# Performer attention with a mixture of experts: row means of three normalisations as product columns, variances as ScalarE squares with row sums, and two buffers for turned tokens

## The chip, the cores and the metric

The kernel runs on one core of a Trainium2 chip. Its engines work side by side, each through its own instructions in order: PE (TensorE, matrix products), DVE (VectorE), ACT (ScalarE), POOL (GpSimd) and SP, which here issues DMAs. They wait for each other through semaphores. The metric is the device time of one execution in microseconds (us), the median of several. All numbers are float32, save in small parts of the expert choice.

## The reference, cut to what matters

There are 4096 tokens of 256 numbers, as 8 sequences of 512. What is computed:

```python
# x: (8, 512, 256)
a = layernorm(x)                                      # norm "a"
q, k, v = a @ Wq.T + bq, a @ Wk.T + bk, a @ Wv.T + bv # 16 heads of 16
kp, qp = softmax_kernel(k), softmax_kernel(q)         # 64 features per head, exp(xp - diag - max) + eps
attn = ((qp @ (kp^T v)) / (qp @ sum(kp))) @ Wo.T + bo
r = layer_norm(a + attn, g2, be2)                     # norm "b"
r = layer_norm(r + relu(r @ W1.T + b1) @ W2.T + b2, g3, be3)   # norm "c"
x = x + layernorm(r)                                  # norm "d"
xf = layernorm(x)                                     # norm "e"
scores = softmax(xf @ gate_w.T)                       # 8 experts
# every expert takes its 512 best tokens: norm, 256 -> 1024 -> 256, weighted, added to xf
x = x + layernorm(xf)
```

For keys the maximum in `softmax_kernel` runs over all 512 tokens and 64 features of a head, so no key can be exponentiated before the whole sequence's features are known. A norm needs each row's mean and variance. Since a row of `r @ W2.T` and its mean are both linear in `r @ W1.T` and so on, the gate's scores are already computed through extra columns of the products (below).

## The kernel before, in words

**Tiles.** 128 tokens lie on the partitions. A block is one sequence: `NB` = 8 blocks of `NT` = 4 tiles. Weights stay in SBUF; `D` = 256, hidden width `FF` = 1024 in `NF` = 8 pieces, `E` = 8 experts.

**Stages.** The attention stage, with the first MLP and the norms a to e, runs up to about 594 us of the profile. The choice of tokens follows, up to about 650, and then the experts with gather, products and scatter.

**Order.** The attention stage's instructions are put out by `planner` (line 187). Each task has an engine, a weight (its expected time), a place (a due time; block b's places lie 66 further on for each block, `COURSE`) and the tasks that it follows. The planner goes through time: of an engine's tasks that can start first, it takes the one with the lowest place. The result is a fixed order for each engine. PSUM buffers are taken as "mm" (three, for most products), "px" (one, for raw features) and "sm" (one).

**The chain of a block**, by tile names and lines. Norm a gives `xnx`. PE turns it (`TX`, line 544), ACT copies it to `xnT` (548), which has one buffer. Products of it give `pk`, `pq` (564) and `pv` (688); ACT makes `kT` and its squares (574, 575) and `v_aug` (699), DVE copies the gate columns out of `pv` (task GA, 707). `pd` and `pnt` (588, 603) are the squared norms. Raw features `pxk` and `pxq` (627) share the one "px" buffer. DVE takes maxima and subtracts (XK: 646, 649), takes the maximum over tiles (`mxt`, 662); POOL reduces it over the partitions (`mxa`, 670), DVE negates it (`nstab`, 677). Then ACT exponentiates keys (724), DVE adds the small constant (KE, 730) and PE forms the context `pc` (744). For queries DVE finds maxima and subtracts (XQ: `sh` 807, `qd` 814), ACT exponentiates (QE, 826), PE turns (`ptq`, 833), ACT copies to `qpT` (844), PE forms `pdiv` and `po` (864, 874), `pr` (909) and, from `atT` (917), `pw` (932). RW (941) adds `pw` to `xnx` in `r1x`. Norm b follows, `TA` (544) and `xaT` (550), the MLP's `ph` (951), `hT` on ACT (956, task PHe) and `pm` (1004), MA (1016) adds `pm` in `r1x`; then the norms c, d and e, and `xf` on ACT (175).

**A norm** is `stats` (two DVE instructions for each tile, lines 153 and 154), `root` (two on POOL for all four tiles, 157 and 158) and an affine of two DVE instructions a tile (166, 169), or a plain one (161), `centre` and `scaled_plus` (180, 183). In `normalisation` the tasks are letter + S, R and A:

```python
def stats(st, mv, src, i):
    nc.vector.bn_stats(st[:, i, :], src[:, 0:D])
    nc.vector.bn_aggr(mv[:, i, :], st[:, i, :])
```

**Gate columns.** Weight tiles carry further columns beside their 256: `wv_sb` 16, `wo_sb` and `w2_sb` 8. So `pv`, `pw` and `pm` carry each token's share of the gate's scores, which norms then only shift and scale: the tasks G0 to G4, small operations on POOL (lines 471 to 512 hold their helpers). XB (1358) is one POOL addition of the attention's bias to the whole block of `xnx`.

**The last block** has nothing after it. `last_mlp` (1155) works it tile by tile: steps L 1 to 4 on DVE (first, second, third, fourth) with a root on POOL after each of the first three. `scores`, turned as `pT` (1438), begins the choice.

## Time and profile before

| what | us |
| --- | --- |
| median of three runs | 897.42 (897.06 to 898.75) |
| the profiled execution, its own time | 899.18 |
| its span | 897.5 |
| mean granted clock of PE | 0.946 of full speed |
| last matmul of the attention stage ends | 581.6 |
| first matmul of the choice (`pT`) | 593.68 |
| two blocks, from a `pk` to that of the next block but one | 138.6 (205.9 to 344.5) |

The profile follows one execution. Of each engine it gives the busy time, and for each instruction the idle time of its engine just before it and what ended that. The groups of instructions give count, busy time and mean length of one; where neighbours overlap in an engine's pipeline, the mean is longer than the time between two starts. "Issue" in the place of a releaser means that the engine waited for nothing that the profile shows. Idle time on an engine that sets nothing costs nothing.

### The profile page before, as it was taken

To read this page: it belongs to the slowest core of one execution; us is meant where nothing else is said; L and a number is where in the kernel's file an instruction comes from. 1 tells how busy PE (TensorE), PEld (TensorE's weight loads), DVE (VectorE), ACT (ScalarE), POOL (GpSimd) and SP (SyncE) were. 2 spreads that over 40 slices of the span, in tenths; PEclk is the share of its full clock that TensorE was granted. 3 is DMA by queue.
4 is the path that set the end of the run, shared out by engine and by line. 5 is a ranking of instruction groups with operands and counts; after the bars stand their busy time and mean duration, and the time that the engine had idled before them with its cause. 6 is when DMAs were issued, how large, how long until landed. Compare 5 with 4: busy or idle time off the path is not lost.

```text
span 897.5 us, 14830 instructions
## 1 busy us (share of the span) xinstructions
PE 799.7 (89%) x5620; PEld 558.2 (62%) x5620; DVE 597.8 (67%) x1631; ACT 353.5 (39%) x638; POOL 330.2 (37%) x548
## 2 busy tenths in 40 slices
PE   4998899899999989999989999911799999999993
PEld 2675585585585676676677578701485766677663
DVE  5568658789678778687888766887822212887233
ACT  3461624454554464373364463300243223322330
POOL 5032003313203213303213302640553666785784
PEclk9998999999999989999999999955699999999997
DMA  9000001202200400400300300174145558998641
GB/s 308 2 2 1 1 1 47 95 3 65 78 1 1 141 3 3 140 2 2 127 16 1 118 3 1 48 258 165 43 111 114 125 104 263 291 283 239 194 105 36
DMA packets 62231, 79.46 MB, mean 89 GB/s; under 512 B 8016, under 2 KB 52304, under 8 KB 62032
## 3 DMA queue, kind: packets, MB, share of 16 engines
q1 hardware_dynamic: 51600, 60.18, 20.2%
q0 software_dynamic: 9856, 17.46, 8.8%
q8 instruction: 44, 0.72, 0.3%
q10 hardware_dynamic: 704, 0.88, 0.3%
q14 instruction: 27, 0.22, 0.1%
HBM read 45.33 MB, written 33.18 MB: 87 GB/s over the span
## 4 chain that ended last, share of the span: by engine, by line
PE 63%; DVE 21%; POOL 6%; issue 6%; ACT 2%; DMA 1%; POOLq 0%; ACTq 0%; DVEq 0%
PE pwe L1730 11%; PE phe L1712 10%; PE pm L1004 7%; PE ph L951 6%; PE pc L744 3%; PE ptq L833 3%; PE pv L688 3%; PE pw L932 2%; PE pk L564 2%; PE pq L564 2%; DVE qd L814 2%; DVE sh L807 2%; PE pxq L627 2%; PE pdiv L864 2%; PE pxk L627 2%
## 5 line engine op out<-in xcount | busy, mean ns | idle before, releaser
L951 PE MATMUL ph<-xaT,w_sb 128*128 128x512 f32 (+1 forms) x288 | 118.3, 553 | 0.2 <-ACT hT L956 0.2
L1712 PE MATMUL phe<-yT,w1e 128*128 128x512 f32 (+1 forms) x288 | 113.1, 549 | 0.0
L1730 PE MATMUL pwe<-w2e,hTe 128*128 128x256 f32 x512 | 112.4, 379 | 0.0
L1004 PE MATMUL pm<-w_sb,hT 128*128 128x264 f32 x448 | 107.6, 389 | 0.0
L1730 PEld LDWEIGHTS pwe<-w2e,hTe 128*128 128x128 f32 x512 | 96.6, 190 | 14.0 <-issue 1.3
L1004 PEld LDWEIGHTS pm<-w_sb,hT 128*128 128x128 f32 x448 | 82.3, 190 | 15.5 <-issue 2.8
L1712 PEld LDWEIGHTS phe<-yT,w1e 128*128 128x128 f32 x288 | 54.7, 192 | 51.7 <-issue 49.6
L951 PEld LDWEIGHTS ph<-xaT,w_sb 128*128 128x128 f32 x288 | 53.4, 191 | 47.9 <-issue 36.6
L956 ACT ACTIVATE hT<-ph,cols_sb 128x512 f32<-128x512 f32 (+1 forms) x72 | 45.7, 638 | 68.3 <-PE ph L951 68.3
L1721 ACT ACTIVATE hTe<-phe,cols_sb 128x512 f32<-128x512 f32 (+1 forms) x72 | 46.1, 640 | 66.5 <-PE phe L1712 66.3
L724 ACT ACTIVATE kp<-kp,nstab 128x256 f32<-128x256 f32 x128 | 53.5, 495 | 32.2 <-DVE nstab L677 32.2
L1609 POOL DMA_INDIRECT y<-xg,idx x32 | 37.9, 1186 | 63.5 <-DVE num L1571 41.2
L1745 DVE SCALAR_TENSOR_TENSOR o<-b2s_sb,gg,o 128x256 f32<-128x256 f32 x32 | 15.5, 483 | 59.6 <-ACT o L1738 41.7
L1623 POOL DMA_INDIRECT accs<-o,idx x28 | 46.6, 1664 | 11.1 <-issue 5.5
L1738 ACT ACTIVATE o<-pwe,gg 128x256 f32<-128x256 f32 x32 | 15.2, 474 | 88.3 <-PE pwe L1730 86.0
L807 DVE TENSOR_REDUCE sh<-pxq 128x8 f32<-128x512 f32 x64 | 40.9, 680 | 11.2 <-PE pxq L627 11.2
L646 DVE TENSOR_REDUCE mxk<-pxk 128x8 f32<-128x512 f32 x64 | 43.6, 681 | 7.0 <-PE pxk L627 7.0
L814 DVE TENSOR_TENSOR qd<-pxq,sh 128x512 f32<-128x512 f32 x64 | 43.0, 687 | 3.7 <-PE ptq L833 1.6
L844 ACT ACTIVATE qpT<-ptq 128x512 f32<-128x512 f32 x64 | 35.2, 595 | 22.2 <-PE ptq L833 21.9
L649 DVE TENSOR_TENSOR kp<-pxk,diag 128x512 f32<-128x512 f32 x64 | 43.6, 680 | 0.0
L157 POOL TENSOR_SCALAR rs_b<-mv_b 128x4 f32<-128x4 f32 (+1 forms) x9 | 2.4, 268 | 111.5 <-DVE mv_b L154 111.5
L744 PE MATMUL pc<-kp,v_aug 128*34 128x128 f32 x512 | 37.4, 296 | 5.6 <-DVE kp L730 5.6
(273 smaller groups left out, 1549.2 us busy)
## 6 DMA issues: line engine op xcount, KB each, us to landing
w1e<-in_f SPq DMA_DIRECT2D x8, 1024.0 KB, 5.9
w2e<-in_f SPq DMA_DIRECT2D x8, 1024.0 KB, 7.3
z<-acc SPq DMA_DIRECT2D x8, 1024.0 KB, 7.6
x<-in_x_in SPq DMA_DIRECT2D x8, 512.0 KB, 6.1
accs<-x SPq DMA_DIRECT2D x8, 512.0 KB, 3.0
acc<-x SPq DMA_DIRECT2D x8, 512.0 KB, 4.5
xg<-xf SPq DMA_DIRECT2D x8, 512.0 KB, 3.6
accs<-xf SPq DMA_DIRECT2D x8, 512.0 KB, 4.2
```

The lines of the kernel that those rows point to most:

```text
L646: nc.vector.tensor_reduce(head_cols(note("mxk", b, [P, NT, H])[:, t, :], c), pxs, AX.X, ALU.max)
L724: nc.scalar.activation(kp[:, :, h, :], kp[:, :, h, :], AF.Exp, bias=nstab[:, h : h + 1])
L744: nc.tensor.matmul(pc[s * 64 : s * 64 + 2 * (DH + 1), i, :], v_aug[:, t, pair, :].rearrange("p h d -> p (h d)"), kp[:, t, pair, :].rearran ...
L807: nc.vector.tensor_reduce(head_cols(kept["sh", b, t], i), pxs[:, :, i, :, :], AX.X, ALU.max,)
L814: nc.vector.tensor_tensor(heads(get("qd", u), c), pxs[:, :, c, :, :], head_cols(kept["sh", b, t], c) .unsqueeze(3).to_broadcast([P, 4, 2, M]),
L951: nc.tensor.matmul(ph, w1_sb[:, c, ts(f, P)], get("xaT", b)[:, c, cols], start=(c == 0), stop=(c == KD - 1),)
L956: nc.scalar.activation(get("hT", b)[:, f, cols], ph, AF.Relu, bias=cols_sb[:, C_B1 + f : C_B1 + f + 1])
L1004: nc.tensor.matmul(kept["PM", b, t, 0], get("hT", b)[:, f, ts(t, P)], w2_sb[:, f, :], start=(f == 0), stop=(f == NF - 1),)
L1623: this = nc.gpsimd.indirect_dma_start(out=table[:, :], out_offset=bass.IndirectOffsetOnAxis(ap=idxs[e][:, j : j + 1], axis=0), in_=src, in ...
L1712: nc.tensor.matmul(ph, w1e[:, c, ts(f, P)], yT[:, c, cols], start=(c == 0), stop=(c == KD - 1))
L1721: nc.scalar.activation(hTs[e][:, f, cols], kept["H", e, f, i], AF.Gelu_apprx_tanh, bias=cols_sb[:, col : col + 1],)
L1730: nc.tensor.matmul(kept["W", e, j], hTs[e][:, f, ts(j, P)], ws[e][1][:, f, :], start=(f == 0), stop=(f == NF - 1),)
```

## The change

The weight tiles get mean columns next to the gate columns: for b one more, c and d two. `r1x` then holds, beside each row, its mean for norm b (column `MB`), c (`MC`) and d (`MD`), made by the same products and shares as the gate's. The mean of e is that of a, since x plus a normalised row keeps its mean. `bn_stats` and `bn_aggr` stay for norm a and for the experts' norms only. For b, c, d and e, DVE scales the means (`less_means`, task N), POOL copies them to where they were (`keep_means`, M), and ACT makes each tile's variance with a Square whose row sum is written out (`variance`, S). `xnT` has two buffers, TX follows the users of two blocks ago instead of one, and a few places change: TX, GA, and PHe, the copies that make `hT`. In `last_mlp` the steps' statistics go the same way (tasks Q on ACT), with `x1` as a temporary. The setup gets small memsets and wider gate products; `gk`, which holds them, is one row. The core of the diff:

```diff
-        wv_sb = wp.tile([P, KD, D + 2 * E], F32, name="wv_sb")
-        wo_sb = wp.tile([P, KD, D + E], F32, name="wo_sb")
+
+
+        MD, MC, MB = E, E + 1, E + 2
+        G3N, G2N = E + 2, E + 3
+        wv_sb = wp.tile([P, KD, D + G2N + E], F32, name="wv_sb")
+        wo_sb = wp.tile([P, KD, D + G2N], F32, name="wo_sb")
         w1_sb = wp.tile([P, KD, FF], F32, name="w1_sb")
-        w2_sb = wp.tile([P, NF, D + E], F32, name="w2_sb")
-        gate3 = wp.tile([P, KD, E], F32, name="gate3")
-        gate2, gate1 = wv_sb[:, :, D : D + E], wv_sb[:, :, D + E :]
-        bo_x = wp.tile([P, 1, D + E], F32, name="bo_x")
+        w2_sb = wp.tile([P, NF, D + G3N], F32, name="w2_sb")
+        gate3 = wp.tile([P, KD, G3N], F32, name="gate3")
+        gate2, gate1 = wv_sb[:, :, D : D + G2N], wv_sb[:, :, D + G2N :]
+        nc.vector.memset(gate3[:, :, MC : MC + 1], 1.0 / D)
+        nc.vector.memset(gate2[:, :, MB : MB + 1], 1.0 / D)
+        part_c = wp.tile([P, 1], F32, name="part_c")
+        nc.vector.memset(part_c, 1.0 / D)
+        bo_x = wp.tile([P, 1, D + G2N], F32, name="bo_x")
...
-        nc.gpsimd.memset(ones_c, 1.0)
+        nc.vector.memset(ones_c, 1.0)
...
-            "xnx": ([P, NT, D + 2 * E], 2), "r1x": ([P, NT, D + E], 3), "x1": (ROWS, 2),
-            "xf": (ROWS, 2), "xnT": (XT, 1), "kT": (XT, 1), "qT": (XT, 1),
+            "xnx": ([P, NT, D + G2N + E], 2), "r1x": ([P, NT, D + G2N], 3), "junk": ([P, D], 1), "x1": (ROWS, 2),
+            "xf": (ROWS, 2), "xnT": (XT, 2), "kT": (XT, 1), "qT": (XT, 1),
...
+        def mean_a(b):
+            return own(small, "ma", b, [P, NT], 3)
...
+            nc.gpsimd.tensor_copy(mean_a(b), mv[:, :, 0])
...
+        def row_means(b, letter):
+
+            if letter == "e":
+                return mean_a(b)
+            col = D + {"b": MB, "c": MC, "d": MD}[letter]
+            return get("r1x", b)[:, :, col]
+
+        def less_means(b, letter, tiles=slice(0, NT)):
+
+            nm = own(small, "nm" + letter, b, [P, NT], 2)
+            nc.vector.tensor_scalar(
+                nm[:, tiles], row_means(b, letter)[:, tiles], -(D ** -0.5), None, ALU.mult
+            )
+
+        def variance(b, letter, t, src):
+
+            nc.scalar.activation(
+                get("junk", 0), src, AF.Square, bias=kept["nm" + letter, b][:, t : t + 1],
+                scale=D ** -0.5, accum_out=ln(letter, b)[1][:, t, 1:2],
+            )
+
+        def keep_means(b, letter, tiles=slice(0, NT)):
+            nc.gpsimd.tensor_copy(
+                ln(letter, b)[1][:, tiles, 0], row_means(b, letter)[:, tiles]
+            )
+
+        def normalisation(b, letter, place, source, behind_, each=None, behind_each=(), means=None):
+
+            if means is not None:
+                task(
+                    (letter + "N", b), "DVE", 0.16, place - 0.5, lambda: less_means(b, letter), means
+                )
+                task(
+                    (letter + "M", b), "POOL", 0.25, place, lambda: keep_means(b, letter), means
+                )
             for t in range(NT):
                 def work(t=t):
                     st, mv, _ = ln(letter, b)
                     stats(st, mv, source()[:, t, :], t)
-                task((letter + "S", b, t), "DVE", 0.58, place + 0.6 * t, work, behind_(t))
+                if means is None:
+                    task((letter + "S", b, t), "DVE", 0.58, place + 0.6 * t, work, behind_(t))
+                else:
+                    task(
+                        (letter + "S", b, t), "ACT", 0.55, place + 0.5 * t,
+                        lambda t=t: variance(b, letter, t, source()[:, t, :]),
+                        [*behind_(t), (letter + "N", b)],
+                    )
             task(
                 (letter + "R", b), "POOL", 1.35, place + 2.5,
...
-                    ("GA", b, t), "DVE", 0.17, 4.7 + 2 * t,
+                    ("GA", b, t), "DVE", 0.17, 2 * t - 8,
...
-                [("GA", b, t) for t in range(NT)] + [("P2", 0), ("G3", b - 2)],
+                [("GA", b, t) for t in range(NT)] + [("P2", 0), ("G3", b - 2), ("eN", b - 3), ("eM", b - 3)],
...
-                (0.96, first), [("BA", 0)],
+                (0.96, first), [("BA", 0)], [("RW", b, t) for t in range(NT)],
...
-                    ("PHe", b, f), "ACT", 0.69, place + 2,
+                    ("PHe", b, f), "ACT", 0.69, place - 14,
...
-                (0.83, residual), [("S1", b - 2)] + [("XF", b - 2, t) for t in range(NT)],
+                (0.83, residual), [("S1", b - 2)] + [("XF", b - 2, t) for t in range(NT)], [("G2", b)],
...
-            normalisation(b, "e", at_ + 16, lambda: get("x1", b), lambda t: [("dA", b, t)])
+            normalisation(b, "e", at_ + 16, lambda: get("x1", b), lambda t: [("dA", b, t)], means=[("G0", b)])
...
+                def mean(letter, t):
+                    return row_means(b, letter)[:, t : t + 1]
                 def first(t=t):
-                    x = r1()[:, t, :]
                     nc.vector.tensor_tensor(
-                        get("r1x", b)[:, t, :], kept["PM", b, t, 0], get("r1x", b)[:, t, :], ALU.add
-                    )
-                    told("c", t, r1())
+                        get("r1x", b)[:, t, 0 : D + G3N], kept["PM", b, t, 0],
+                        get("r1x", b)[:, t, 0 : D + G3N], ALU.add,
+                    )
+                    less_means(b, "c", slice(t, t + 1))
                     nc.vector.scalar_tensor_tensor(
-                        x, x, one("c", t)[0][:, 0, 0:1], row(G3), ALU.subtract, ALU.mult
+                        get("x1", b)[:, t, :], r1()[:, t, :], mean("c", t), row(G3),
+                        ALU.subtract, ALU.mult,
                     )
                 def second(t=t):
-                    x = r1()[:, t, :]
-                    scaled_plus(x, x, one("c", t)[1], 0, row(BE3))
-                    told("d", t, r1())
-                    centre(x, x, one("d", t)[0], 0)
-                    share(in_r1(b)[:, t, :], one("c", t)[0][:, 0, 0:1], ns3, one("c", t)[1], k3)
+                    rs = ln("c", b)[2][:, t : t + 1]
+                    share(in_r1(b, MD + 1)[:, t, :], mean("c", t), ns3, rs, k3)
+                    less_means(b, "d", slice(t, t + 1))
+                    x = get("x1", b)[:, t, :]
+                    scaled_plus(x, x, rs, 0, row(BE3))
+                    nc.vector.tensor_scalar(r1()[:, t, :], x, mean("d", t), None, ALU.subtract)
                 def third(t=t):
+                    rs = ln("d", b)[2][:, t : t + 1]
+                    if t == 0:
+                        less_means(b, "e")
                     scaled_plus(
-                        get("x1", b)[:, t, :], r1()[:, t, :], one("d", t)[1], 0, x0s[b][:, t, :]
-                    )
-                    told("e", t, get("x1", b))
-                    share(
-                        in_r1(b)[:, t, :], one("d", t)[0][:, 0, 0:1], ns1, one("d", t)[1],
-                        note("x0g", b, None)[:, t, :],
-                    )
+                        get("x1", b)[:, t, :], r1()[:, t, :], rs, 0, x0s[b][:, t, :]
+                    )
+                    share(in_r1(b, E)[:, t, :], mean("d", t), ns1, rs, note("x0g", b, None)[:, t, :])
                 def fourth(t=t):
-                    (mv, rs), nb = one("e", t), note("nbe", b, [P, NT])
+                    nb = note("nbe", b, [P, NT])
                     nc.vector.scalar_tensor_tensor(
-                        nb[:, t : t + 1], mv[:, 0, 0:1], -1.0, rs, ALU.mult, ALU.mult
-                    )
-                    share(in_r1(b)[:, t, :], mv[:, 0, 0:1], ns1)
+                        nb[:, t : t + 1], mean("e", t), -1.0, ln("e", b)[2][:, t : t + 1],
+                        ALU.mult, ALU.mult,
+                    )
+                    share(in_r1(b, E)[:, t, :], mean("e", t), ns1)
...
-                    (1, 1.48, first, "c"), (2, 1.75, second, "d"), (3, 1.4, third, "e"),
-                    (4, 0.34, fourth, None),
+                    (1, 1.0, first, "c"), (2, 1.25, second, "d"), (3, 0.8, third, "e"),
+                    (4, 0.3, fourth, None),
...
+                            ("Q", b, t, step), "ACT", 0.55, at_ + 3 + 2.5 * step,
+                            lambda t=t, letter=letter: variance(
+                                b, letter, t, (r1() if letter == "c" else get("x1", b))[:, t, :]
+                            ),
+                            [("L", b, t, step)],
...
-                b, "TX", -14, lambda b=b: get("xn", b), lambda b=b: get("xnT", b),
+                b, "TX", -18, lambda b=b: get("xn", b), lambda b=b: get("xnT", b),
                 [("aA", b, t) for t in range(NT)],
-                [("V", b - 1, t) for t in range(NT)] + [(n, b - 1, c) for n in "kq" for c in range(KD)],
+                [("V", b - 2, t) for t in range(NT)] + [(n, b - 2, c) for n in "kq" for c in range(KD)],
```

## The prediction, made before the run

> **What bounds it.** I read the page's busy shares first, then the table of windows over the attention stage, then PE's waits, then the timelines around those waits.
>
> ```profile
> PE 799.7 (89%) x5620; PEld 558.2 (62%) x5620; DVE 597.8 (67%) x1631; ACT 353.5 (39%) x638; POOL 330.2 (37%) x548
> ...
> 0.00:66.00 66.00, 52.76 (x480) 37.08 (x481) 41.08 (x101) 31.98 (x57) 19.73 (x44) 0.95 0.31 106
> 66.00:130.00 64.00, 58.38 (x538) 40.59 (x538) 43.65 (x104) 26.24 (x48) 8.15 (x15) 0.95 0.01 1
> ...
> 195.00:260.00 65.00, 62.66 (x506) 42.86 (x502) 52.87 (x141) 34.19 (x62) 17.69 (x37) 1.00 0.16 50
> ```
>
> A window's columns are bounds, length, busy time of PE, weight loads, DVE, ACT, POOL, then granted clock. Inside the blocks PE is busy 62.7 of 65 us, DVE 53, ACT 34. The six windows from 130 to 520 add to 374.3 of 390: only 15.7 us are to be gained there, however much DVE loses. From PE's first instruction at 11.62 to 130 us it idles 54.4 + 64 − 52.76 − 58.38 = 7.2 us. What the idle time waits for, between 130 and 545 us:
>
> ```profile
> PE pxq L627 <- DVE qd L814: 7.2, 3, 3.4
> PE pc L744 <- DVE kp L730: 5.4, 6, 1.7
> PE ptq L833 <- ACT qd L826: 2.3, 1, 2.3
> PE pd L588 <- ACT xaT L550: 1.0, 3, 0.3
> ...
> DVE nstab L677 <- POOL mxa L670: 21.8, 6, 4.9
> ...
> POOL mxa L670 <- issue: 36.9, 6, 6.4
> ```
>
> With the small ones it is 17.5 us over six blocks, 2.9 a block. 14.9 of it is one place: the stretch where keys wait for nstab, and it is POOL that is late there. One instance in the timelines (start, duration):
>
> ```profile
> 235.88 0.25 POOL L513 TENSOR_TENSOR x0g<-x0g,gm 128x32 f32<-128x32 f32 x1
> 242.15 0.39 POOL L670 PARTITION_ALL_REDUCE mxa<-mxt  x1 [6.01 <-issue]
> ...
> 234.62 0.25 DVE L662 TENSOR_REDUCE mxt<-mxk 128x16 f32<-128x64 f32 x1
> ...
> 242.57 0.17 DVE L677 TENSOR_SCALAR nstab<-mxa 128x16 f32<-128x16 f32 x1 [3.23 <-POOL mxa L670]
> ```
>
> mxt is done at 234.87, yet mxa starts 7.3 us later: 6 us after POOL's previous operation ended. All six instances read 6.0 to 6.4 "issue". The first mxa of the kernel, with POOL long idle, follows mxt by 0.13 us, so the six are spent after POOL's last operation, not after the data. The planner places nothing for them.
>
> **The change, part by part.** *DVE loses* the statistics of four norms of five, 16 tiles a block:
>
> ```profile
> L153 DVE BATCH_NORM_STATS2 st_b<-r1x 128x6 f32<-128x256 f32 x32 | 13.7, 427 | 1.1
> L154 DVE BATCH_NORM_AGGREGATE mv_b<-st_b 128x2 f32<-128x6 f32 x32 | 5.8, 182 | 1.1
> ...
> L175 ACT ACTIVATE xf<-x,nbe,rs_e 128x256 f32<-128x256 f32 x32 | 17.3, 591 | 17.8 <-DVE nbe L1278 10.9 <-DVE nbe L1114 6.8
> ```
>
> A pair starts every 0.53 us: 16 × 0.53 = 8.5 us a block; four mean scalings of about 0.2 come back. *ACT gains* 16 Squares with row sums. No ACT row has a row sum. Lower bound, the same shape without one: 0.59 alone, four in 2.07, so 0.52 apart. For the sum, DVE shows the nearest thing:
>
> ```profile
> 595.58 0.43 DVE L1477 SCALAR_TENSOR_TENSOR junk_h<-kh,one_c 128x256 bf16<-128x256 f32 x1
> 595.93 0.09 DVE L1477 DVE_READ_ACCUMULATOR junk_h<-kh,one_c 128x1 bf16 x1
> ```
>
> There a separate read of 0.09 follows. On ACT I take 0.60 apart (0.52 + 0.09), upper end 0.73 (0.52 plus ACT's smallest operation, 0.21, L1035): 9.6 us a block onto ACT's 34. ACT stays under 70%.
>
> [...] The longest new chain is b's, from the last pw to TA: RW with its hop 0.65, mean 0.2, four Squares, root 1.35, four affines 3.7. [...] I take the row, with 0.55 us a block for small stalls around TA and pnt, since kT, v_aug and nT now queue on ACT behind Squares that wait for d's and b's means.
>
> *Mean columns.* pm is 266 wide for 264, pw 267, pv 275 for 272. Their matmuls overlap, so I scale the busy time, not the mean: PE is busy 107.6 us on pm (seven blocks), 14.7 on the last block's, 32.0 on pw, 34.9 on pv. 122.3 × 2/264 + 32.0 × 3/264 + 34.9 × 3/272 = 0.93 + 0.36 + 0.38 = **+1.7**, all on PE, so all on the path. Lower end 0, if the extra columns hide in the pipeline. The added memsets fall in DVE's idle first 2.2 us; no DMA is moved.
>
> *Order in the steady blocks.* The built order runs every block alike, where before odd and even ones differed. With T the end of the second pxk: before, nstab came at T+13.0 and T+15.2 (229.6 to 242.57, 296.9 to 312.13), since the gate copies stood behind XK on DVE and XB behind them on POOL. Now the copies come first: XB T+0.3 to 2.7, G0 with its new copies to T+4.3, the 6.1 us, nstab T+10.4. But on DVE nstab now stands ahead of three statistics pairs of a and of all of XQ(0), part of which stood ahead of it: 1.6 + sums 1.5 + two qd 1.2 + two or three KE 0.9 + QE 1.05 + hops = 6.4 us to the first ptq. PE's cover from T is ph 6.87, pxq 1.1, pm 7.12 = 15.1, so ptq waits 10.4 + 6.4 − 15.1 = 1.7; pc 0.35; around TA 0.55. Together 2.6 against 2.9: −0.3 a block, **−1.8** over six.
>
> *POOL's new work* is five small copies a block, 0.25 each; one stands before mxa and is in the 4.3. XB holds DVE up only in rare cases: nbe took 2.16 us beside it once, at 301.32, and XK beside it kept its 0.68.
>
> *Second xnT and earlier hT.* TX moves ahead, between pr and pw of the block before, with its copies on ACT; hT's are ranked higher. Both waits for xnT (0.7 before pk, 0.7 before pt_TX) go. Of the first blocks' other waits (0.53, 1.03, 0.67, 0.44, 0.44, 0.21, 1.58, 0.71, between 75 and 105 us) the last two go with the order; but block 1 has new ones at pxq, held by XK, and at TA, which has no cover there yet. Net **−2.5**, bounds −5 and +2.
>
> *Last block.* Its pw_2 and pw_3 stand before TA, which has nothing beside it: two c affines stand ahead of atT on DVE (about 1.6) less what was waited there before: **+1.5**, bounds 0 and 3.
>
> *Tail.* The last matmul of the stage ends at 581.6:
>
> ```profile
> 583.90 0.43 DVE L1254 TENSOR_TENSOR r1x<-pm,r1x 128x264 f32<-128x264 f32 x1
> ...
> 593.68 0.66 PE L1438 MATMUL pT<-ident,scores 128*128 128x128 f32 x2 [12.08 <-DVE scores L1041]
> ```
>
> The last tile's first step starts 2.3 us late, behind block 6's work and tile 2's steps on DVE. These lose their statistics, so it can start at 0.3. Three Squares with hops enter the chain, about what three pairs take out. 12.1 becomes 9.5: **−2.6**, bounds −4 and 0. The MoE stage is the same code.
>
> Sum: −2.5 − 1.8 + 1.7 + 1.5 − 2.6 = −3.7. The profiled execution took 899.18, span 897.5; it would take 895.5. It lay 1.76 over the median of the runs, which becomes **893.7**. A measurement of this kernel can tell about 0.2% (1.8 us) from no change.
>
> **Rivals.** (1) *Slower: a late nstab decides each block.* XB needs the fourth gate copy. If DVE reaches that copy only behind one and a half XK pairs (1.2 us each), XB, G0, the six microseconds and nstab all move by 1.9, to T+12.3, and ptq waits 3.6. That is 11.4 over six blocks: 893.7 + 11.4 = **905**. It decides from nstab at T+11.0, where 0.6 × 6 eats the 3.7. For it: 21.8 us of DVE already wait for mxa, and nothing now stands between nstab and a full queue of XQ. Against: copies and XB come 2.4 us earlier in the order. Chance 0.33. (2) *Much faster:* DVE, lighter by 8 us a block, answers every wait for kp and qd: 12.6 of the 17.5 us go, and the sum is −3.7 + 1.8 − 12.6 = −14.5, **883**. Against: those waits begin with POOL, which gets more work. Chance 0.17. (3) *No gain:* DVE's time was hidden, the orders' stalls change places, and only tail, xnT, last block and widening are left: −2.6 − 1.4 + 1.5 + 1.7 = −0.8, **896.6**. For it: PE's 96% in the blocks. Chance 0.15. The forecast has 0.35.
>
> Faster is the forecast with most of its spread, and rival 2: 0.33 + 0.17 = 0.50. Within 0.2%: 0.14. Slower: 0.36. The range 883 to 905 reaches both outer rivals; the forecast's own is 889 to 896.
>
> **What would show it.** DVE's busy time in a 65 us window falls by about 7, ACT's rises by 9; L153 and L154 keep only a in the blocks. [...] nstab near T+10.4 with 6 us "issue" before mxa, ptq waiting for qd about 1.7: if 3 or more, rival 1. pT's wait near 9.5. A stall of PE on kT or v_aug behind Squares would prove my ACT account wrong.

## The result, and the profile after

The changed kernel takes 902.84 us (median of six runs, 901.60 to 903.96) against 896.59 (894.09 to 898.75) for the kernel before on the same chip: **1.0074 of its time, 95% interval 1.0053 to 1.0095**. It is slower by 0.7%. The forecast was 893.7, faster.

The page's busy line of the changed kernel, and its table of windows over the same stretches as in the prediction:

```profile
PE 804.5 (89%) x5624; PEld 559.3 (62%) x5624; DVE 536.4 (60%) x1419; ACT 420.6 (47%) x894; POOL 329.6 (37%) x585
...
0.00:66.00 66.00, 49.54 (x356) 33.11 (x356) 36.96 (x96) 25.57 (x48) 19.27 (x45) 0.90 0.31 106
66.00:130.00 64.00, 59.12 (x580) 41.61 (x578) 43.42 (x99) 33.67 (x65) 8.35 (x18) 0.92 0.01 1
...
195.00:260.00 65.00, 63.34 (x515) 43.08 (x515) 44.47 (x112) 41.43 (x93) 17.82 (x43) 1.00 0.15 50
```

The work moved as meant: in the third row DVE has 44.5 us instead of 52.9 and ACT 41.4 instead of 34.2, and PE idles 1.7 us instead of 2.3. The first row says where to look: PE has done 3.2 us less by 66 us, and its granted clock there is 0.90 instead of 0.95. What PE waits for in the attention stage:

```profile
PE pT L1524 <- DVE scores L1106: 9.3, 1, 9.3
PE ptq L897 <- ACT qd L890: 8.7, 5, 2.6
PE pxq L691 <- DVE kp L713: 5.1, 2, 4.4
PE pw L996 <- DVE atT L981: 4.1, 1, 4.1
PE pxq L691 <- DVE qd L878: 3.9, 1, 3.9
```

Three waits of about 4 us each are new, and each stands once: pxq for qd at 58.35 us (block 0), pxq for kp at 89.82 (block 1), pw for atT at 554.55 (the last block). The steady blocks have nothing of the kind.

With the starts of `pct` (one early product in each block) as marks, the two profiled executions, 899.18 and 902.65 us, split like this:

| stretch | before | after | difference | forecast |
| --- | --- | --- | --- | --- |
| start to block 1's pct | 112.2 | 118.8 | +6.6 | -2.5 |
| block 1's pct to block 7's (steady) | 422.5 | 415.2 | -7.3 | -1.8, and most of the widening's +1.7 |
| block 7's pct to the stage's last matmul | 46.9 | 54.8 | +7.9 | +1.5 |
| from there to pT | 12.1 | 9.3 | -2.8 | -2.6 |
| pT to the end | 303.8 | 302.9 | -0.9 | 0 |

The steady blocks gave far more than was forecast, and both ends of the stage, where PE has no other block's work beside it, took more than that back. (Part of the 7.3 us is luck of the clock; more on this where the prediction is judged.) (0.7 of the 6.6 us is PE's later start, at 12.29 instead of 11.62, which lies between 11.1 and 12.3 from kernel to kernel.)

### The profile page after: what moved, and what is told of

It reads as the page before. It is cut to its first block, busy times and chain, and to the rows that moved or that the text cites. A ratio compares the mean times of both kernels' runs of the same rounds, so it can differ in the third digit from the quotient of the medians.

```text
span 901.0 us, 14966 instructions
## 1 busy us (share of the span) xinstructions
PE 804.5 (89%) x5624; PEld 559.3 (62%) x5624; DVE 536.4 (60%) x1419; ACT 420.6 (47%) x894; POOL 329.6 (37%) x585
## 4 chain that ended last, share of the span: by engine, by line
PE 70%; DVE 17%; issue 6%; POOL 3%; ACT 3%; DMA 1%; POOLq 0%; ACTq 0%; DVEq 0%
PE pwe L1816 11%; PE phe L1798 10%; PE ph L1015 8%; PE pm L1068 6%; PE pw L996 4%; PE ptq L897 3%; PE pk L628 3%; PE pv L752 3%; PE pc L808 3%; PE pq L628 3%; DVE mxk L710 2%; PE pxk L691 2%; DVE kp L713 2%; PE pdiv L928 2%; DVE qd L878 2%
## 5 line engine op out<-in xcount | busy, mean ns | idle before, releaser
L1015 PE MATMUL ph<-xaT,w_sb 128*128 128x512 f32 (+1 forms) x288 | 116.1, 555 | 0.6 <-ACT xaT L1286 0.6
L1068 PE MATMUL pm<-w_sb,hT 128*128 128x266 f32 x448 | 106.7, 389 | 0.0
L908 ACT ACTIVATE qpT<-ptq 128x512 f32<-128x512 f32 x64 | 36.1, 592 | 23.2 <-PE ptq L897 22.8
L897 PE MATMUL ptq<-ident,qd 128*128 128x128 f32 x256 | 37.2, 280 | 9.0 <-ACT qd L890 8.7
L890 ACT ACTIVATE qd<-qd 128x1024 f32<-128x1024 f32 x32 | 33.8, 1055 | 16.6 <-DVE qd L878 16.5
```

Source lines behind the costliest of these rows:

```text
L897: nc.tensor.transpose(pt[:, i, :], get("qd", u)[:, 2 * hp : 2 * hp + 2, :].rearrange("p h m -> p (h m)"), ident,)
L1015: nc.tensor.matmul(ph, w1_sb[:, c, ts(f, P)], get("xaT", b)[:, c, cols], start=(c == 0), stop=(c == KD - 1),)
L1068: nc.tensor.matmul(kept["PM", b, t, 0], get("hT", b)[:, f, ts(t, P)], w2_sb[:, f, :], start=(f == 0), stop=(f == NF - 1),)
```

## Experiments

The kernels of a group ran on one chip and share its runs of the kernel before: the four from ga_first, the four from prime, the four from after_again, and the last three. Chips differ by some microseconds (the kernel before took 896.15 to 902.06 us in the four groups), so only the ratios are compared across groups, and small differences between groups are read with care. Line numbers in a changed kernel lie up to four further on.

| kernel | median us | before, same chip | ratio (95%) |
| --- | --- | --- | --- |
| ga_first | 904.07 | 902.06 | 1.0031 (1.0008 to 1.0054) |
| ga_last | 907.37 | 902.06 | 1.0089 (1.0053 to 1.0125) |
| ga_both | 907.88 | 902.06 | 1.0073 (1.0045 to 1.0101) |
| before_ga | 911.25 | 902.06 | 1.0124 (1.0094 to 1.0154) |
| prime | 897.56 | 896.15 | 1.0009 (0.9990 to 1.0028) |
| prime_first | 896.64 | 896.15 | 0.9996 (0.9977 to 1.0015) |
| no_row_sums | 897.65 | 896.15 | 1.0023 (1.0000 to 1.0047) |
| one_xnT | 899.31 | 896.15 | 1.0015 (0.9995 to 1.0035) |
| after_again | 907.57 | 901.93 | 1.0079 (1.0049 to 1.0108) |
| prime_first_xb | 900.84 | 901.93 | 0.9988 (0.9967 to 1.0010) |
| prime_two_xb | 902.75 | 901.93 | 1.0010 (0.9989 to 1.0031) |
| prime_places | 962.76 | 901.93 | 1.0685 (1.0655 to 1.0716) |
| prime_b0 | 894.90 | 902.02 | 0.9920 (0.9889 to 0.9951) |
| before_prime | 900.02 | 902.02 | 0.9985 (0.9956 to 1.0014) |
| phe_back | 937.77 | 902.02 | 1.0389 (1.0333 to 1.0445) |

### Is it the order of the gate copies?

The first theory blamed the moved place of the gate copies (GA): in the first and the last block nothing is left over that could fill PE. Three kernels give the old place back to block 0, to the last block, or to both; a fourth moves only this place in the kernel before.

```diff
-                    ("GA", b, t), "DVE", 0.17, 2 * t - 8,
+                    ("GA", b, t), "DVE", 0.17, 2 * t - (8 if b else -4.7),               # ga_first
+                    ("GA", b, t), "DVE", 0.17, 2 * t - (8 if b < NB - 1 else -4.7),      # ga_last
+                    ("GA", b, t), "DVE", 0.17, 2 * t - (8 if 0 < b < NB - 1 else -4.7),  # ga_both
```

```diff
-                    ("GA", b, t), "DVE", 0.17, 4.7 + 2 * t,
+                    ("GA", b, t), "DVE", 0.17, 2 * t - 8,                                # before_ga
```

> The changed kernel with the gate copies of block 0 alone at their old place (4.7 + 2t; the other blocks keep 2t - 8); the planner then puts the first two blocks of PE in the order of the kernel before. Theory A (the loss is the order of the first two blocks and of the last, and half clock after the stalls there; the Squares gain): the second po of block 1 starts near 128 to 129 us instead of 134.5, and the time falls by about 6, to 896 to 898. Theory B (Squares with row sums, 0.60 us a tile on ACT instead of 0.53 on DVE, cost their time in every block): no gain beyond 1 us, 902.

> The changed kernel with the gate copies of the last block alone at their old place; the planner then lets the last pw stand between the ph of the last MLP, as before. A: the 4.1 us wait of pw for atT and its slow matmuls (3.93 us for eight instead of 2.04) go; the last matmul of the stage ends about 4.5 us earlier, time 897.5 to 899. B: no change beyond 1 us, 902.

> Both: gate copies of blocks 0 and 7 at their old place, those of 1 to 6 at the new one. A: both gains add, 902.8 - 6 - 4.5 = about 892, below the kernel before (896.6). B: 901 to 902.

> The kernel before with nothing changed but the place of the gate copies, 2t - 8; no Squares, no mean columns, one buffer for turned tokens. PE's order of the first two blocks is then all but that of the changed kernel. A: the first two blocks lose 5 to 7 us here too, the second po of block 1 starts at 133 to 135 us instead of 127.9; the order of the other blocks shifts as well, so the time is 898 to 905. B: the same as before within 2 us, 895 to 898.

**Block 0: yes, in part.** In ga_first block 0's pct starts at 57.2 instead of 67.2, as early as in the kernel before (58.5). But block 1's pct comes at 115.3, not 10 us earlier: from one mark to the next it takes 58.1 us where the changed kernel takes 51.6 and the kernel before 53.8. Something else makes block 1 long. By the ratios (1.0031 against 1.0074) ga_first gains some 4 us of the 6 expected. before_ga, with nothing but this place changed, also loses in the first blocks (block 1's pct at 116.6 instead of 112.2), and at 1.0124 it is slower than theory A allowed. ga_both, with both ends in the old order, has 1.0073, the changed kernel's own ratio; about 0.995 was expected.

**Last block: no.** ga_last gains nothing (1.0089). PE has the order of before there, and the stall only changes place, to TA. Its rows of PE's waits, and POOL's timeline (start, duration, in brackets the idle time before it and what ended it):

```profile
PE pt_TA L1276 <- DVE r1x L169: 5.0, 2, 4.6
```

```profile
544.72 0.19 POOL L564 COPY mv_b<-r1x 128x2 f32<-128x2 f32 x1 [25.68 <-DVE r1x L1005]
551.84 0.24 POOL L157 TENSOR_SCALAR rs_b<-mv_b 128x2 f32<-128x2 f32 x1 [6.94 <-issue]
```

POOL copies the means in 0.19 us, and then stands for 6.94 us before the root that every affine needs. The wait is "issue": it stands for no data. That is a better suspect than any order.

### POOL's seven microseconds after mxa

The same place in the changed kernel. POOL's timeline:

```profile
519.37 0.39 POOL L734 PARTITION_ALL_REDUCE mxa<-mxt  x1 [6.65 <-issue]
519.65 0.28 POOL L1123 COPY sg<-scores 128x32 f32<-128x32 f32 x1
543.41 0.19 POOL L564 COPY mv_c<-r1x 128x4 f32<-128x4 f32 x1 [23.48 <-DVE r1x L1080]
551.07 0.25 POOL L157 TENSOR_SCALAR rs_c<-mv_c 128x4 f32<-128x4 f32 x1 [7.47 <-issue]
```

and of the kernel before:

```profile
518.25 0.39 POOL L670 PARTITION_ALL_REDUCE mxa<-mxt  x1 [6.14 <-issue]
518.53 0.28 POOL L1058 COPY sg<-scores 128x32 f32<-128x32 f32 x1
546.81 0.25 POOL L157 TENSOR_SCALAR rs_b<-mv_b 128x2 f32<-128x2 f32 x1 [28.01 <-DVE mv_b L154]
```

Before mxa there are the known six microseconds. There are some seven more **after** it, ahead of the first operation that isn't a plain copy: the sg copy follows mxa at once. In the kernel before, this operation was a root. POOL came to it early, waited 28 us for data, and the root ran as soon as mv_b was there, so the seven microseconds must lie inside the 28. In the changed kernel a **copy** of row means stands ahead of the root. It waits 23.48 us for norm c's means, runs without a pause, and only then do the seven microseconds begin, with the last block's norms waiting. If that is so, any small operation right after mxa takes them into the idle time:

```diff
+        primed = wp.tile([P, NT], F32, name="primed")
...
-                lambda: nc.gpsimd.partition_all_reduce(
-                    note("mxa", b, [P, H]), note("mxt", b, None), P, bass_isa.ReduceOp.max
+                lambda: (
+                    nc.gpsimd.partition_all_reduce(
+                        note("mxa", b, [P, H]), note("mxt", b, None), P, bass_isa.ReduceOp.max
+                    ),
+                    nc.gpsimd.tensor_scalar(primed, mhalf, 1.0, None, ALU.mult),
                 ),
```

Nothing reads `primed`. prime is the changed kernel with it; before_prime, the control, is the kernel before with it.

> The changed kernel with one small POOL operation (a 128x4 tensor_scalar into a tile of its own) right after each mxa, nothing else. Theory P: in the last block the new mean copy of norm c is the first thing on POOL after mxa; it waits 23 us for its data, and the 7.5 us that POOL needs before its next other operation start only then, in front of rs_c, atT and pw. With the small operation they pass while POOL is idle: rs_c at about 543.9 on the scale of the changed kernel instead of 551.1, PE's 4.1 us wait before the last pw under 1, its eight matmuls 2.0 us instead of 3.9, last pm about 5 earlier, ratio to before 1.001 to 1.003 instead of 1.0074. Theory O (the order of the last block: atT behind four affines on DVE): the wait stays at 3 or more, ratio 1.006 to 1.008.

> The kernel before with the same small POOL operation after each mxa. If what prime gave back is the wait that the mean copy had put in front of POOL's 7 us in the last block, it gives nothing here, where those microseconds lie in idle time already: ratio 0.998 to 1.002. If the small operation helps for another reason (every block's POOL), this kernel gains as well, 0.993.

POOL's waits of prime from 100 us on, its timeline at the same place, and PE's wait for atT:

```profile
POOL primed L739 <- issue: 51.0, 7, 7.7
```

```profile
543.71 0.19 POOL L565 COPY mv_c<-r1x 128x4 f32<-128x4 f32 x1 [15.23 <-DVE r1x L1084]
547.12 0.24 POOL L157 TENSOR_SCALAR rs_c<-mv_c 128x4 f32<-128x4 f32 x1 [3.21 <-ACT junk L559]
```

```profile
PE pw L1000 <- DVE atT L985: 1.2, 1, 1.2
```

The small operation costs POOL 51 us of waiting in seven blocks, and the kernel gets **faster** for it: rs_c no longer waits for issue, pw waits 1.2 us instead of 4.1, and the stage's last matmul ends at 583.97 instead of 588.79. rs_c comes at 547.12, not at the expected 543.9: it now waits 3.21 us for the last Squares on ACT. The ratio falls from 1.0074 to 1.0009, intervals apart, though on different chips. The traces don't need the chips to agree: from block 7's pct to the stage's last matmul, the five kernels with `primed` and the moved places (prime, prime_first, prime_first_xb, prime_two_xb, prime_b0) take 49.7 us each, and the seven without `primed` that keep hT's new place 53.5 to 56.3. In the kernel before the same operation moves nothing that the interval shows (0.9985, 0.9956 to 1.0014), which fits: there no copy stands ahead of the root.

Four microseconds of waiting cost more than four. The windows of the changed kernel around that wait (PE's busy time is the first figure after the length; the clock is the third from the end):

```profile
545.00:550.00 5.00, 4.65 (x78) 3.84 (x79) 2.30 (x6) 3.43 (x12) 0.00 (x0) 1.00 0.01 3
550.00:553.00 3.00, 0.44 (x4) 0.25 (x3) 0.50 (x2) 0.00 (x0) 1.85 (x4) 0.95 0.00 0
553.00:555.00 2.00, 0.45 (x1) 0.45 (x2) 1.85 (x4) 0.00 (x0) 1.68 (x6) 0.50 0.00 0
555.00:557.00 2.00, 2.00 (x6) 1.46 (x6) 1.45 (x4) 0.00 (x0) 1.76 (x6) 0.50 0.01 4
557.00:559.00 2.00, 2.00 (x8) 1.50 (x6) 0.71 (x3) 0.00 (x0) 0.12 (x1) 0.50 0.00 0
```

Half clock sets in during the wait, at 552.7 us, and lasts 6.8 us, and the eight pw after it take 3.93 us; the eight before it took 2.04. In the attention stage of the changed kernel half clock comes in stretches of 3.4, 6.8 or 10.2 us. The three long waits (3.93, 4.11 and 4.40 us) all have it behind them, 6.8, 6.8 and 10.2 us of it. But waits of only 2.64 us (ptq at 186.3) and 1.79 us (322.6) have 3.4 us of half clock behind them as well, and those of 1.42 and 1.64 us have none. What brings it on and what ends it no run shows.

### What the Squares, the second buffer and the places are worth

Four kernels ask what the parts of the change do. no_row_sums takes the row sums off the Squares of blocks 0 to 6 and sets their variances to 1.0 with a small POOL memset, so it leaves the variances of these blocks out; one_xnT gives back the single buffer with TX's old place and its waits; phe_back gives hT's copies their old place; prime_places gives back all the moved places and the one buffer, and so keeps means, Squares and `primed` alone.

```diff
-                scale=D ** -0.5, accum_out=ln(letter, b)[1][:, t, 1:2],
+                scale=D ** -0.5,
+                accum_out=ln(letter, b)[1][:, t, 1:2] if b == NB - 1 else None,  # no_row_sums
...
+            if b < NB - 1:
+                nc.gpsimd.memset(ln(letter, b)[1][:, tiles, 1], 1.0)             # no_row_sums
```

```diff
-            "xf": (ROWS, 2), "xnT": (XT, 2), ...
+            "xf": (ROWS, 2), "xnT": (XT, 1), ...          # one_xnT, prime_places
-                b, "TX", -18, ...
-                [("V", b - 2, t) ...
+                b, "TX", -14, ...                         # one_xnT, prime_places
+                [("V", b - 1, t) ...
-                    ("PHe", b, f), "ACT", 0.69, place - 14,
+                    ("PHe", b, f), "ACT", 0.69, place + 2,   # phe_back, prime_places
-                    ("GA", b, t), "DVE", 0.17, 2 * t - 8,
+                    ("GA", b, t), "DVE", 0.17, 4.7 + 2 * t,  # prime_places
```

> The changed kernel with the row sums left out of the Squares of blocks 0 to 6 (the variance is set to 1.0 by a small POOL memset in the task of the mean copy; the Squares stay, so the variances of these blocks are left out of the computation). It shows what the separate reading of the sums costs: 16 x 0.19 us of ACT a block. If ACT sets the pace in the blocks (theory B) the period falls by 1 to 3 us, the time by 7 or more. If they lie beside PE's work (theory A) the blocks 2 to 6 keep 67 to 68 us; block 1, where norm b's chain has no cover, gains 0.3 to 0.8; time within 2 us of the changed kernel.

> The changed kernel with one buffer for turned tokens and TX at its old place. PE's order of the blocks 2 to 6 stays as it is. If the second buffer is worth what I put on it (0.7 + 0.7 at the start) the time rises by 1 to 2 us; since TX, pk and pq were late only there, I expect no change beyond the noise of 2 us.

> The changed kernel with the place of hT's copies back at +2 (it was moved to -14), nothing else. prime_places took 61 us more than before, with PE waiting 8 to 10 us for QE's qd in each block, since no pm stands there. If hT's place is what puts pm_0 and pm_1 in front of ptq, this kernel shows the same: 55 to 65 us slower than before, ratio 1.05 to 1.07. If it is the gate copies or TX: 1.005 to 1.01.

> The mean columns and Squares alone: every changed place back (TX, gate copies, hT), one buffer for turned tokens, and the small POOL operation after mxa. By theory A the core of the change gains in the steady blocks only with its order; here every block stands with TA between pq and pq, and QE's wait for qd comes at ptq each time: a period of 68 to 70 us. First blocks near those of before plus 2 (b's chain). Ratio 0.996 to 1.004. If the Squares cost time in every block: 1.006 or more.

**The row sums don't set the pace.** Without them a steady block (pct of block 2 to pct of block 6, a quarter of it) takes 67.7 us; with them 67.8. By the ratios (1.0023 against 1.0074, on different chips) no_row_sums is some 4 us below the changed kernel, more than the 2 us expected; in the traces its block 1 is 1.9 us shorter and its stretch from block 7's pct to the last matmul 1.3, so what it gains is at the ends, and part of that is a stretch of half clock that it lacks. On ACT the sums can be seen. Its groups by form, of the changed kernel up to 600 us:

```profile
L558 ACT ACTIVATE junk<-r1x,nmb 128x256 f32<-128x256 f32 x32 | 16.3, 508 | 13.0 <-DVE nmb L552 10.9 <-DVE nmd L552 1.3
...
L558 ACT ACTIVATION_READ_ACCUMULATOR junk<-r1x,nmb 128x1 f32 x32 | 6.0, 187 | 0.0
```

Each Square is followed by a read of 0.19 us, as DVE's are by one of 0.09. Squares of one norm start 0.63 us apart (86.13, 86.76, 87.40, 88.03); the forecast had 0.60.

**The second buffer gains nothing here**: 1.0015 (0.9995 to 1.0035) with one, where the change with two has 1.0074 and 1.0079, on two other chips; the changed kernel itself did not run on this one. Blocks 2 to 6 have the same order in both; block 1 is 2.7 us shorter with one buffer (75.2 from its pct to the next, against 77.9), and no_row_sums, with two buffers, has 76.0. The traces show most of the difference: after its ptq wait of 2.64 us the changed kernel has half clock from 187.5 to 190.9 us, which costs 1.7 us; in one_xnT this wait is 1.55 us and in no_row_sums 2.28, and the 32 products pc behind it take 2.12 and 2.11 us there, where the changed kernel's take 3.12.

**The moved places are what makes the Squares bearable.** With all of them back the kernel takes 1.0685 of before's time, and a steady block 78.5 us. That was a miss: 0.996 to 1.004 and 68 to 70 us were expected. PE's waits of prime_places, and below of phe_back:

```profile
PE ptq L901 <- ACT qd L894: 57.8, 7, 10.1
```

```profile
PE ptq L897 <- ACT qd L890: 33.0, 6, 8.7
```

PE comes to ptq with no pm ahead of it and waits through the whole of nstab and qd, up to 10.1 us at a time. hT's copies alone make about half of it: their place decides how many products PE has in hand while POOL goes through its six microseconds. phe_back's loss has the direction expected and is smaller than expected (1.0389, not 1.05 to 1.07). So the places are no mere tidying beside the Squares. What no run tests is the other side: all moved places in the kernel before, with its DVE statistics (before_ga moves only GA). How much of the steady blocks' gain is due to the Squares, and how much to the order alone, stays open.

### The first two blocks

after_again repeats the changed kernel on another chip, as the measure for its group. prime_first is prime with ga_first's line. prime_first_xb lets XB of a block wait until the affines of the block before are done; prime_two_xb has that too, and the old GA place for blocks 0 and 1. prime_b0 has the old GA place for blocks 0 and 1, `primed`, and norm b of block 0 by the old DVE statistics.

```diff
-                [("TX", b, 0), ("TX", b, 1), ("BA", 0)] + [("GA", b, t) for t in range(NT)],
+                [("TX", b, 0), ("TX", b, 1), ("BA", 0)] + [("GA", b, t) for t in range(NT)]
+                + ([("bA", b - 1, t) for t in range(NT)] if b else []),       # prime_first_xb, prime_two_xb
```

```diff
-                    ("GA", b, t), "DVE", 0.17, 2 * t - 8,
+                    ("GA", b, t), "DVE", 0.17, 2 * t - (8 if b > 1 else -4.7),    # prime_two_xb, prime_b0
...
-                (0.96, first), [("BA", 0)], [("RW", b, t) for t in range(NT)],
+                (0.96, first), [("BA", 0)], [("RW", b, t) for t in range(NT)] if b else None,   # prime_b0
```

> The same, and the gate copies of block 0 at their old place. Both losses off: the gain of the blocks between (1.2 to 1.8 us each, five of them) is left, less what block 1 still pays for the longer chain of norm b. Ratio 0.993 to 0.998, below the kernel before. If the Squares cost time in every block, it stays at or above 1.000.

> The changed kernel once more, unchanged, beside the others on one chip, since the kernel before took 894 to 905 us on another chip. Ratio to before 1.004 to 1.008; PE's 4.1 us wait before the last pw and POOL's 7 us in front of rs_c in the last block are there again.

> The run prime_first, and XB of a block waits for the affines of norm b of the block before. Theory L: in prime_first XB (2.44 us on POOL from 82.88) held one affine of b on DVE for 2.37 us instead of 0.48, and with it TA, PE's 2.3 us wait and the half clock after it. With XB behind the affines they take 0.5 each, TA waits 0.4 to 0.5 three times, the pct of block 1 comes at 116 or earlier instead of 118.7; ratio 0.994 to 0.998. Theory C (it is norm b's longer chain over ACT and POOL that TA waits for): TA still waits 2 us or more in one piece, ratio 0.999.

> As prime_first_xb, with the gate copies of block 1 at their old place as well, so that the first two blocks stand nearly as in the kernel before, with the Squares in them. If the places made the loss of the first blocks, their pct comes near 58.5 and 112 to 114 as before; if the Squares' chain makes it, 116 or later. Ratio 0.991 to 0.997 by the first.

> The changed kernel with the small POOL operation after mxa, the gate copies of blocks 0 and 1 at their old place, and norm b of block 0 alone by bn_stats on DVE again (its means and variances as before; all other norms b to e stay Squares). PE's first two blocks then stand as in the kernel before. Theory C (norm b's chain over DVE, POOL and ACT is 2.1 us longer from the last RW to the root, and has no cover in block 1): pct of blocks 0 and 1 near 58.5 and 112 to 114 us, TA's longest wait under 1; with the steady gain kept, ratio 0.990 to 0.995, below the kernel before. If something else costs the first blocks: pct of block 1 at 116 or later, ratio 0.998 or more.

prime_first reaches the time of before, 0.9996, and not the 0.993 to 0.998 expected: its block 1 is long as in ga_first, 60.0 us from pct to pct. Its timeline in that block, of DVE, POOL and PE in turn:

```profile
82.70 0.49 DVE L166 SCALAR_TENSOR_TENSOR r1x<-r1x,mv_b,rows_sb 128x256 f32<-128x256 f32 x1
83.23 2.37 DVE L169 SCALAR_TENSOR_TENSOR r1x<-r1x,rs_b,rows_sb 128x256 f32<-128x256 f32 x1
...
82.88 2.44 POOL L1448 TENSOR_TENSOR xnx<-xnx,bo_x 128x1068 f32<-128x1068 f32 x1
...
85.65 0.47 PE L609 MATMUL pt_TA<-ident,r1x 128*128 128x128 f32 x1 [2.33 <-DVE r1x L169]
```

Beside XB an affine takes 2.37 us instead of 0.49: the earlier gate copies bring XB onto the affines, and PE waits 2.33 us. XB ends at 85.32, and the affine at 85.60. Why the affine is longer beside XB no run shows. With XB behind the affines (prime_first_xb) no TA waits over 0.51 us. Yet the qd that PE waits for later in the block comes only 0.4 us sooner (its ptq starts at 107.20 instead of 107.63, with a wait of 4.1 us instead of 3.5); block 1's pct is 1.8 us earlier (116.9 instead of 118.7), most of it through a shorter stretch of half clock (the 32 products pc behind that wait take 2.56 us instead of 3.63). The ratio, 0.9988, can't be told from prime_first's, and misses the 0.994 to 0.998 expected.

prime_two_xb shows the rest, with nearly before's order for both blocks. Its pct stand at 58.2 and 119.4 us and its ratio is 1.0010, as expected if the chain of Squares makes the loss. The last sum of residual rows, POOL's root of norm b, and PE's TA behind it:

```profile
77.15 0.44 DVE L1009 TENSOR_TENSOR r1x<-pw,xnx 128x267 f32<-128x267 f32 x1
...
80.42 0.22 POOL L157 TENSOR_SCALAR rs_b<-mv_b 128x4 f32<-128x4 f32 x1 [2.58 <-ACT junk L559]
...
83.11 0.44 PE L609 MATMUL pt_TA<-ident,r1x 128*128 128x128 f32 x1 [2.91 <-DVE r1x L169]
```

and in the kernel before:

```profile
77.36 0.42 DVE L941 TENSOR_TENSOR r1x<-pw,xnx 128x264 f32<-128x264 f32 x1
...
78.55 0.22 POOL L157 TENSOR_SCALAR rs_b<-mv_b 128x4 f32<-128x4 f32 x1 [20.16 <-DVE mv_b L154]
```

The last sum of residual rows starts 3.27 us before the root in prime_two_xb, and 1.19 us before it in the kernel before: the chain with four Squares at its end is **2.1 us longer** than the chain whose statistics run tile by tile as pw comes in. In later blocks PE has the block before's MLP beside it. Here there is none. TA's 2.91 us are not all: later in the block pxq waits another 2.91 us for qd.

prime_b0 undoes that for this one norm. PE's waits for TA up to 592 us:

```profile
PE pt_TA L609 <- DVE r1x L169: 1.6, 3, 0.6
```

It takes 894.90 us where the kernel before takes 902.02 on the same chip: **0.9920 (0.9889 to 0.9951)**, the only kernel whose interval lies below 1. The Squares stay in all other blocks. `primed` in the kernel before gave 0.9985 (0.9956 to 1.0014), and every run of prime_b0 (891.94 to 896.98) lies below every run of before_prime (897.15 to 903.50) on the same chip, so it isn't the small operation alone.

Ratio and TA's waits are as expected, the marks are not. Block 0's and block 1's pct come at 61.0 and 116.8 us; 58.5 and 112 to 114 were expected, and 116 or later was to mean another cause. In part the mark itself has moved: PE does two groups of eight pm ahead of block 1's pct here, the kernel before and prime_two_xb one (about 2 us). In part it is half clock, which takes 5.1 us ahead of block 0's pct where it takes 3.4 in the kernel before. Block 2's pct, at 191.2, is 6.0 us earlier than in prime_two_xb (197.2), with 6.0 us less idle time on PE, and still 2.1 later than in the kernel before (189.1). So norm b's chain cost some 6 us of waits there (prime_b0 also drops the rule for XB), and taking it out does not quite restore the first blocks. What makes prime_b0 the faster kernel lies between the pct of blocks 2 and 7: 334.3 us, where before_prime on the same chip has 340.1.

What stays open is the part of each cause in the 6.6 us of the changed kernel. From 10 to 140 us, PE's idle time and what half clock took (busy time times one minus the clock, in windows of 1 us) sum to 8.8 + 6.3 = 15.1 us in the kernel before, 11.3 + 10.7 = 22.0 in the changed one and 8.0 + 8.2 = 16.2 in prime_b0. The difference of 6.9 is block 1's lateness, and over half of it is clock. But where the slow stretches fall differs between runs: ga_first and ga_both have the same order in block 0, and their pct start at 57.2 and 60.8. A microsecond of waiting has no fixed price there.

## Why the prediction was wrong

*What bounds the kernel*: right. PE is bound, and its waits sum in the steady blocks from 17.5 us to 11.0 (ptq 8.7, pnt 1.4, pxq 0.7, pc 0.2).

*Steady blocks*: the mechanism was right and close in its times. In the instance at 236 us nstab came 10.7 us after the second pxk (forecast 10.4), mxa after 6.63 us of issue, the first ptq 6.1 us after nstab's end (6.4), with a wait of 1.42 (1.7). Five waits of this kind sum to 8.7 us. The term was mis-sized in its small parts: 0.35 a block for pc was 0.2 in all six. No run shows the 0.55 a block around TA and pnt, an estimate of the author's: pnt waited 1.4 us in all, TA not at all. So the stalls fell by 6.5 us instead of 1.8. Another 2.8 of the stretch's 7.3 us are clock (the widening works against both), which no term foresaw: half clock costs 6.2 us there in the kernel before and 3.4 in the changed one. That part is luck. before_prime, the kernel before but for one small operation, has 1.6 and takes 417.2 us instead of 422.5; after_again on the same chip takes 413.3. Rival 1, a late nstab, did not happen; its price, 905, is near the time for other reasons.

*ACT's Squares*: 0.63 apart instead of 0.60, inside the bounds, but by a misread row. The four `xf` start 0.49 apart, not 0.52 (2.07 us is the whole length of four), and `xf` takes both bias and scale from tiles, a Square only its bias. A Square's read starts 0.42 us after it, and the next Square 0.21 after that; the read takes 0.19, twice the 0.09 taken from DVE. Where PE had another block beside it, b's chain stayed covered: from 130 to 545 us PE has no wait for TA.

*Widening*: +1.7 was on the high side. PE's busy time went from 107.6 to 106.7 on pm, from 34.9 to 36.1 on pv and from 32.0 to 34.9 on pw, of which 1.9 is the slow eight of the last block. That leaves 1.3.

*XB*: it held up nbe three times in the kernel before (2.38, 2.16 and 2.16 us, at 161.41, 301.32 and 439.83), not once; the affine beside it in prime_first, 2.37 us instead of 0.49, is the same case.

*Tail*: right, 9.29 us against 9.5.

*First two blocks*: **the step that failed first**, -2.5 against +6.6. It counted the small waits that the second xnT and the new order remove, and took block 1's new ones for a part of "net". It didn't follow block 0 at all, where the order puts PE before the second pxq with DVE's qd still to be done and no other work in hand, and it gave b's chain there no price of its own, although it said that TA has no cover in block 1 yet. It had no term for the clock, which the table of windows already showed at 0.95 in these windows.

*Last block*: **the second**, +1.5 against +7.9. "Two c affines ahead of atT" was the right place, and the wait there was 4.1 us. What it took for a queue on DVE was a root that POOL could not begin: the new copies of means were costed at 0.25 us each, and nothing was said of what the copy keeps back. prime took 5.1 of the 7.9 us away: 2.9 of the wait, and the rest what half clock had cost after it. Of the 2.8 left, 2.1 are PE's waits (1.25 and 0.51 before pw, 0.21 before pr and 0.56 before ph, where the kernel before has one of 0.42), and 0.7 is more work on PE.

The upper end of the range, 905, held the time, but by rival 1's wrong reason. The chances did not lean that way: both ends of the stage were treated as corrections to a steady state, and they decided.

## What to carry to other kernels

Norm b's chain, 2.1 us longer, cost PE no wait for TA where another block's work stood beside it (130 to 545 us of the changed kernel), and 2.91 us in one piece where none did (block 1 of prime_two_xb). So a chain that is made longer has to be priced again, chain by chain, in the first and last block; there the old form can stay, as prime_b0 keeps it for one norm. Before a small operation is added to an engine, look at what that engine used to do unseen while it waited: the new operation can push it into the open, as the copy of means did here with POOL's 7.47 us. PE's wait of 4.11 us before the last pw cost 6 with the clock after it: the eight pw behind it took 3.93 us instead of 2.04.

## What the runs showed of the hardware

- POOL stands about 7 us ("issue", 6.8 to 7.7) before the first operation after PARTITION_ALL_REDUCE that isn't a plain copy, besides the 5.8 to 7.6 before it. Copies ran without it (sg, 0.28 us directly behind mxa). In the changed kernel it began only when that operation was next in line (7.47 us behind the copy of mv_c), and in the kernel before that operation waited 28.01 us for its data and had no issue in front of it; before_prime, with `primed` at that place, has 7.11 us of issue there. What POOL does in it no run shows.
- An ACTIVATE with a row sum is two instructions: 128x256 took about 0.51 us, the read of the sum 0.19, and such pairs start 0.63 apart.
- In the changed kernel half clock (0.50 in the windows) followed PE's waits of 3.9 to 4.4 us and lasted 6.8 to 10.2 us: 32 products pc took 3.63 us at 60.37 and 1.94 at 52.48. It also came with next to no wait: in the kernel before from 39.0 to 42.4 and from 49.3 to 52.7 us, each time behind a row of pg products of 8 to 16 columns, with PE busy but for one wait of 0.21 us. Whether the narrow products bring it on, no run tests.
- A DVE operation of 0.16 us (nbe) took 2.2 to 2.4 beside XB, three times in the kernel before and once in the changed one.
